# Four products of a block pair placed on four column quarters of TensorE, and small operands widened to all rows and columns

## The chip, the core and the metric

The kernel runs on one core of a Trainium2 chip. The metric is the device time of one execution in microseconds (us); of several runs the median is given. One execution was also recorded by the hardware profiler, and all durations below come from that record.

## What is computed

A two-layer graph network on 2708 nodes with 256 features. `adj` is 2708 x 2708, with about 3 in 1000 entries set near the average column and many more for the first nodes. Layer 0 (diagonal of the adjacency taken out as `dn`):

```python
node_support = node_adj_norm @ h
edge_output = _gru_cell(node_support, h, ...)
# per head:
hW = h @ W
hp = (node_adj > 0).astype(hW.dtype) @ hW
hm = (node_adj < 0).astype(hW.dtype) @ hW
e_plus = jax.nn.leaky_relu(jnp.concatenate([hp, hm], axis=1) @ a, ALPHA)[:, 0]
att = softmax(where(edge_adj > 0, e_plus[None, :], NEG_INF), axis=1)
out_head = att * edge_adj @ hW          # three heads, averaged
node_output = _gru_cell(edge_support, h, ...)
x = _layernorm(x + de[:, None] * edge_output + dn[:, None] * node_output)
```

Layer 1 is a graph attention of four heads over the entries of `adj` above 0.5 (`alpha = softmax(leaky_relu(s_src + s_dst), axis=0)`, `out = einsum(alpha, h)`), again with a residual and a layer norm.

## The kernel before

The nodes are cut into 22 blocks of 128 (the last has 20) and six groups of 512 columns (the last has 148). Everything is written as a list of operations that a planner (`Plan`, lines 99 to 276) orders by itself: each operation gets a cost (`cost`, line 151) and a `table`. On ScalarE that is an activation table; on TensorE, line 218, it is 1 for f32 operands and 2 for bf16. When the planner picks the next operation of an engine, one of another table counts as less urgent by `STAY` (5 us on TensorE) and costs `SWITCH` (0.13 us) more. Consecutive TensorE calls into the same tile are joined to one operation (`note`, line 192), up to 16. The order on each engine's queue, SP's and GpSimd's too, is the one that `issue` (line 230) finds. All instructions carry line 219 in the profile, so they are told apart by tile names.

The work goes in three stages.

*The pass* (lines 874 to 942) reads the transposed adjacency once, for each of the six groups in 11 pairs of blocks, 128 rows x 512 columns each. For a pair, ScalarE writes `over2` (sign of entry - 0.5) and `mask2` (sign of the entry, diagonal taken out by GpSimd), VectorE finds which 64-column pieces hold entries (`found0`). TensorE then makes four bf16 products: for each block b, `only[:, b, :]` (22 columns, a one in column b) with `over2`, summed into bank `dbs[0]` (`pf`), and `u3[:, b, :]` (9 columns: three heads in three bf16 parts) with `mask2`, into bank `accs[0]` (`pe`). At the end of a group, `logits` copies `pe` to `e9` and transposes it by a product with `sum3`; `flags` compares `pf` with `least` into `into` and transposes that with `ident_h`. Both read the banks that the next group writes. In between, `keep` (line 855) makes f32 products of x with the recurrent weights (`w_hs`), 128 x 512, into banks `accs[1]` and `dbs[1]` and stores them to `f_XH`; `listed` and `spread` turn the found blocks into index lists by bf16 products (`ls`, `pl` from `ids`). GpSimd gathers columns of the adjacency by these lists. After the last group, `head_weights` writes the exponentials into `f_T` (T0), and only then can rows be gathered from there.

*Layer 0* (lines 1238 to 1249) goes over 43 column blocks of 64. For each of some 181 gathered tiles GpSimd fetches `rows`, ScalarE scales the adjacency tile into `four` (three heads and the plain one) and writes its sign into `m0`, TensorE multiplies `rows` with `four` in f32 (`multiplied`) into `sums`, and every four tiles makes four small bf16 products of `m0` (64 columns) with 9 weights into `dens`. `divided` sums these, inverts them, spreads them over 64 x 192 (`rden_own`) and multiplies with `ones_f`, from 64 rows. After each group of 512 columns, `cells_and_norm` runs the GRU cells in f32 (`side`), the norm, and `projected` for layer 1.

*Layer 1* (lines 1401 to 1405) gathers from `f_T1` and is not touched.

What sets the order around the change: `over` and `mask` have three buffers each, the adjacency pairs five or six, so ScalarE's activations wait for TensorE's products three pairs back, and SP's loads for ScalarE and VectorE.

Of the kernel before, what the change touches and what calls it, by code (L numbers as in the profile page):

```python
# [20 lines left out]
P = 128  # L21
# [77 lines left out]
class Plan:  # L99
# [51 lines left out]
    def cost(self, engine, method, out, ins, kwargs):  # L151

        n = max(self.count(v) for v in [out] + ins)
        if method == "indirect_dma_start":
            return 1.25, 4.5
        if method == "dma_start":
            size = 4
            for _, k in tuple(out.ap):
                size *= k
            return 0.08 if engine == "sync" else 0.25, self.LOAD + size / self.RATE  # L160
        if engine == "tensor":
            n, rows = self.count(out), ins[0].ap[-1][1]
            if ins[0].dtype == BF16:
                t = max(0.035, n / 2400)
            elif method == "transpose":
                t = 0.11
            else:
                t = max(0.22 if rows <= C1 + 1 else 0.26, n / 595)
            return t, t + 0.1
        by_partition = any(isinstance(kwargs.get(k), bass.AP) for k in ("bias", "scale"))  # L170
        if engine == "scalar":
            t = 0.09 + n / 1200 + 0.1 * by_partition
        elif engine == "gpsimd":
            t = 0.1 + n / (1300 if method == "memset" else 320)
        elif method == "reciprocal":
            t = 0.07 + n / 160
        else:
            pairs = all(v.dtype == BF16 and tuple(v.ap)[-1] == (1, 2) for v in [out] + ins)
            t = 0.06 + n / (1900 if pairs else 3800 if method == "memset" else 960)
            t += 0.065 * (method == "scalar_tensor_tensor")  # L180
        return t, t + 0.08

    def note(self, engine, method, f, args, kwargs):
# [33 lines left out]
        if engine == "tensor":  # L217
            table = 1 + (ins[0].dtype == BF16)
        call = lambda: f(*args, **kwargs)  # L219
# [89 lines left out]
def fast_path(ctx: ExitStack, tc: tile.TileContext, i: dict, out: bass.AP, bad: bass.AP):  # L309
# [107 lines left out]

    only = const.tile([P, NB, NB], BF16, name="f_only")
    nc.gpsimd.memset(only, 0.0)
    for b in range(NB):  # L420
        nc.gpsimd.memset(only[:, b, b : b + 1], 1.0)

# [27 lines left out]
    for t, of in ((less_room, TILES0 + TILES1), (less_whole, WHOLE0 + WHOLE1)):  # L450
# [7 lines left out]

    least = const.tile([NB, 1], F32, name="f_least")
    nc.vector.tensor_scalar(  # L460
        least, ident[:NB, last : last + 1], float(P - size[last]), 0.5 - P, op0=ALU.mult, op1=ALU.add
    )

    sum3 = const.tile([H3, HEADS0], F32, name="f_sum3")
    nc.vector.tensor_add(sum3, ident[:H3, 0:3], ident[:H3, 3:6])
    nc.vector.tensor_add(sum3, sum3, ident[:H3, 6:9])
    sum9 = const.tile([H3, HEADS0], F32, name="f_sum9")
    nc.vector.tensor_scalar(sum9, sum3, float(HEADS0), None, op0=ALU.mult)

# [130 lines left out]
    def spread(layer, cs, rows, row_f, place):  # L600
# [29 lines left out]
        for b in range(NB):  # L630
            p = size[b]
            nc.tensor.matmul(
                pl[: 2 * rows * n, : n * PLACES], lhsT=lhs[:p, b // 2, b % 2], rhs=hot[:p, :, b // 2, :, b % 2],
                start=(b == 0), stop=(b == last),
            )
# [59 lines left out]
    ap, tiles = Rings(const, 1, home2), Rings(const, 8, home1)  # L695
    u3 = ap.tile([P, NB, H3], BF16, name="f_u3")
    e_col = const.tile([P, NB, HEADS0], F32, name="f_e_col")
# [93 lines left out]
    def logits(g, pe):  # L791

        e9 = ap.tile([H3, CH], F32, name="e9", bufs=2)
        w, bl = width[g], groups[g]
        nc.scalar.copy(e9[:, :w], pe[:H3, :w])
        pc = side()
        for n, b in enumerate(bl):
            nc.tensor.matmul(
                pc[: size[b], n * HEADS0 : (n + 1) * HEADS0],
                lhsT=e9[:, n * P : n * P + size[b]], rhs=sum3, start=True, stop=True,  # L800
            )
        full = sum(size[b] == P for b in bl)
        v = pc[:, : len(bl) * HEADS0].rearrange("p (b h) -> p b h", h=HEADS0)
        if full:
            nc.vector.tensor_copy(e_col[:, bl[0] : bl[0] + full, :], v[:, :full, :])
        if full < len(bl):
            nc.vector.tensor_copy(e_col[: size[last], last:, :], v[: size[last], full:, :])
# [20 lines left out]
    def flags(g, pf):  # L828

        into = ap.tile([NB, CH], BF16, name="into", bufs=2)  # L830
        w, bl = width[g], groups[g]
        nc.vector.tensor_scalar(into[:, :w], pf[:NB, :w], least, None, op0=ALU.is_gt)
        pt = side()
        for n, b in enumerate(bl):
            nc.tensor.matmul(
                pt[: size[b], n * NB : (n + 1) * NB], lhsT=into[:, n * P : n * P + size[b]],
                rhs=ident_h[:NB, :NB], start=True, stop=True,
            )
        full = sum(size[b] == P for b in bl)
        v = pt[:, : len(bl) * NB].rearrange("p (b c) -> p c b", c=NB)  # L840
        if full:
            nc.vector.tensor_copy(flags1[:, :, bl[0] : bl[0] + full], v[:, :, :full])
        if full < len(bl):
            p = size[last]
            nc.vector.tensor_copy(flags1[:p, :, last:], v[:p, :, full:])
# [28 lines left out]
    for g, cs in enumerate(groups):  # L874
        w = width[g]
        pe, pf = accs[0], dbs[0]
        c0, nf = base[g] // W0, w // W0
        for b0 in range(0, NB, 2):
# [30 lines left out]
            for p, s in parts:  # L909
# [7 lines left out]
                if nf * W0 < w:  # L917
# [4 lines left out]
                    )  # L922
            for b in pair:
                p = size[b]
                nc.tensor.matmul(
                    pf[:NB, :w], lhsT=only[:p, b, :], rhs=over2[:p, b - b0, :w], start=(b == 0), stop=(b == last)
                )
            for b in pair:
                p = size[b]
                nc.tensor.matmul(  # L930
                    pe[:H3, :w], lhsT=u3[:p, b, :], rhs=mask2[:p, b - b0, :w], start=(b == 0), stop=(b == last)
                )
        logits(g, pe)
        flags(g, pf)
        if g == NG - 3:
# [32 lines left out]

    COUNTED = 4
    gp, zp = Rings(const, 2, home1), Rings(const, 1, home2)  # L970

# [21 lines left out]
    def prepared(n):  # L993
# [16 lines left out]
        for h in range(HEADS0):  # L1010
            nc.scalar.activation(four[:, (h + 1) * w : (h + 2) * w], a, AF.Copy, scale=weight[:, h : h + 1])
        m0 = sp.tile([P, W0], BF16, name="m0", bufs=2 * COUNTED)
        nc.scalar.activation(m0[:, :w], a, AF.Sign)
# [11 lines left out]
    def multiplied(n):  # L1025
# [10 lines left out]
        for o in range(KD):  # L1036
# [3 lines left out]
            )  # L1040
        counted.append((start, stop, m0[:, :w], e3))
        if stop or len(counted) == COUNTED:
            for first_of, last_of, mask, weights_of in counted:
                nc.tensor.matmul(
                    dens[c][:w, :H3], lhsT=mask, rhs=weights_of, start=first_of, stop=last_of,
                    skip_group_check=True,
                )
            counted.clear()
# [5 lines left out]
    def divided(c):  # L1054
# [4 lines left out]
        acc = sums[c]  # L1059
        rden = small.tile([W0, HEADS0], F32, name="rden")[:w]  # L1060
        rb = small.tile([P, HEADS0 * W0], F32, name="rb")[:, : HEADS0 * w]
        own = small.tile([W0, HEADS0, W0], F32, name="rden_own")[:w, :, :w]

        if at == 0:
            zs[g] = (
                zp.tile([P, KD, CH], F32, name="sa", bufs=2), zp.tile([P, HEADS0, KD, CH], F32, name="z")
            )
        none = small.tile([W0, HEADS0], F32, name="none0")[:w]
        nc.vector.tensor_reduce(
            rden, dens[c][:w, :H3].rearrange("p (s h) -> p h s", s=3), AX.X, ALU.add  # L1070
        )
# [8 lines left out]
        nc.vector.tensor_mul(  # L1080
            own, ident[:w, :w].rearrange("p (o i) -> p o i", o=1).to_broadcast([w, HEADS0, w]),
            rden.rearrange("p (h o) -> p h o", o=1).to_broadcast([w, HEADS0, w]),
        )
        pb = dens[c][:, P : P + HEADS0 * w]
        nc.tensor.matmul(pb, lhsT=ones_f[:w], rhs=own, start=True, stop=True, skip_group_check=True)
        nc.scalar.copy(rb, pb)
# [6 lines left out]
    def cells_and_norm(g):  # L1093
# [87 lines left out]
        def projected(b):  # L1181
# [9 lines left out]
            of_head = ah[:, :H65].rearrange("p (h c) -> p h c", h=HEADS1)  # L1191
            s = small.tile([P, 2 * HEADS1], F32, name="s_d")[:p]
            nc.vector.tensor_scalar(s, ph[:p, D : D + 2 * HEADS1], REACH1, -REACH1, op0=ALU.min, op1=ALU.max)
            nc.scalar.activation(of_head[:, :, C1 :], s[:, :HEADS1].rearrange("p (h o) -> p h o", o=1), AF.Exp)
            nc.scalar.activation(ah[:, H65:], s[:, :HEADS1], AF.Exp, scale=SLOPE - 1.0)
            nc.tensor.transpose(pd[:HEADS1, b * P - c0 : b * P - c0 + p], s[:, HEADS1:], ident[:p, :p])
            nc.vector.tensor_mul(
# [19 lines left out]

        pd = dbs[1] if g == NG - 1 else ls_bank()
        for b in bl:
            projected(b)  # L1220
        S = small.tile([HEADS1, CH], F32, name="S", bufs=1)
        nc.scalar.activation(S[:, :w], pd[:HEADS1, :w], AF.Exp, scale=1.0 - SLOPE)
# [638 lines left out]
```

## Time and profile before

| | |
|---|---|
| three runs, us | 877.8, 881.07, 885.95 (median 881.07) |
| profiled execution | 877.66, its span 875.8 |
| matmuls on TensorE, busy | 780.4 us (89%), 3911 instructions |
| weight loads | 490.4 us (56%) |
| VectorE, ScalarE, GpSimd busy | 609.9 (70%), 551.3 (63%), 532.3 (61%) |
| GpSimd's gathers of `rows` | 254, 258.0 us, 1.016 each |
| f32 products of `rows` with `four` | 712 records, mean 400 ns |
| bf16 products of the pass | 132 into `acc`, 132 into `db` |

In the trace each f32 product shows as two matmul records. [...] two neighbours overlap and the sum of durations is more than the time they take; the distance from one start to the next is the better measure. "128*22" in a row is the product's rows and columns of weights, "128x512" the operand that streams through. "[idle <-X]" and "<-X" name what ended a wait. The stages meet at about 225 us (last column sums of the pass) and 700 us (last cells of layer 0).

### The profile page before, as it was taken

What the parts mean: (1) busy time and instruction counts of PE and PEld (TensorE: products, weight loads), DVE (VectorE), ACT (ScalarE), POOL (GpSimd) and SP (SyncE); (2) the same over time, 40 slices, a digit from 0 to 9 for tenths busy, and PEclk for the clock granted to TensorE, in tenths of its full rate; (3) what the DMA queues carried; (4) which work ended last, traced back from release to release, by engine and by line L of the source; (5) the groups of instructions that cost most, each with busy time, mean ns of one, the idle gap of its engine ahead of it and who ended that gap; (6) DMA issues with size and microseconds to landing.
All of it is one profiled execution on the core that took longest, in us unless ns stands there. A gap on an engine that the chain in (4) does not pass through costs nothing. (4 is left out here: it accounts for less than half of the span.)

```text
span 875.8 us, 14092 instructions
## 1 busy us (share of the span) xinstructions
PE 780.4 (89%) x3911; PEld 490.4 (56%) x3911; DVE 609.9 (70%) x2063; ACT 551.3 (63%) x1560; POOL 532.3 (61%) x613
## 2 busy tenths in 40 slices
PE   4999998997999999988998997999999899998882
PEld 3533333444556764656555744754664588777761
DVE  6259585865846674978478638727857849999993
ACT  3368997975568885658456844745764432237887
POOL 3000557557667777777777777777776243677630
PEclk9989999998999999989999999999999799999995
DMA  9476887878683342453446425434534143565531
GB/s 345 135 236 209 277 263 241 288 242 243 204 235 98 106 128 56 135 147 105 112 143 198 126 65 159 126 96 118 159 103 123 29 141 94 172 187 171 169 98 53
DMA packets 88503, 138.71 MB, mean 158 GB/s; under 512 B 21904, under 2 KB 44264, under 8 KB 87776
## 3 DMA queue, kind: packets, MB, share of 16 engines
q1 hardware_dynamic: 67168, 90.56, 32.2%
q0 software_dynamic: 20320, 45.59, 19.7%
q10 hardware_dynamic: 928, 1.57, 0.5%
q8 instruction: 33, 0.54, 0.3%
q14 instruction: 54, 0.44, 0.2%
HBM read 116.18 MB, written 24.26 MB: 160 GB/s over the span
## 5 line engine op out<-in xcount | busy, mean ns | idle before, releaser
L219 POOL DMA_INDIRECT rows<-f_T,f_idx x254 | 258.0, 1016 | 115.9 <-PE acc L219 26.8
L219 PE MATMUL acc<-four,rows 128*128 128x256 f32 (+1 forms) x712 | 187.9, 400 | 8.8 <-ACT four L219 5.7
L219 ACT ACTIVATE four<-four,rows 128x64 f32<-128x64 f32 (+1 forms) x534 | 143.3, 336 | 23.0 <-DMA rows<-f_T,f_idx 15.8
L219 PEld LDWEIGHTS acc<-four,rows 128*128 128x128 f32 x712 | 131.6, 196 | 45.8 <-ACT four L219 14.2
L219 POOL DMA_INDIRECT raw<-in_adj_dram,f_idx x91 | 90.5, 995 | 40.7 <-DVE f_m L219 15.3
L219 POOL DMA_INDIRECT f_xn<-in_adjT_dram,f_idx x63 | 66.8, 1060 | 20.1 <-issue 16.6
L219 POOL DMA_INDIRECT f_home<-in_adjT_dram,f_idx x67 | 66.4, 991 | 20.3 <-issue 16.3
L219 PE MATMUL acc<-f_home,rows 128*65 128x128 f32 (+2 forms) x512 | 65.2, 279 | 3.9 <-ACT f_home L219 2.6
L219 DVE TENSOR_TENSOR f_home<-f_home,side 128x512 f32<-128x512 f32 (+1 forms) x64 | 41.9, 658 | 32.4 <-PE side L219 31.2
L219 PEld LDWEIGHTS acc<-f_home,rows 128*65 128x65 f32 (+1 forms) x512 | 55.7, 140 | 9.6 <-ACT f_home L219 3.5
L219 PE MATMUL side<-f_home,f_gat_w 128*128 128x512 f32 (+1 forms) x144 | 58.7, 569 | 2.0 <-DVE f_home L219 1.9
L219 PE MATMUL side<-f_home,f_node_wi 128*128 128x512 f32 (+1 forms) x144 | 59.1, 543 | 1.3 <-DVE f_home L219 1.3
L219 ACT ACTIVATE m<-four 128x64 bf16<-128x64 f32 (+1 forms) x181 | 40.2, 246 | 28.1 <-DVE four L219 24.0
L219 PE MATMUL side<-f_home,f_edge_wi 128*128 128x512 f32 (+1 forms) x144 | 57.4, 544 | 0.0
L219 DVE SCALAR_TENSOR_TENSOR f_home<-pl,rows,f_m 128x128 f32<-128x128 f32 x196 | 55.2, 335 | 0.0
L219 POOL DMA_INDIRECT f_m<-in_adjT_dram,f_idx x33 | 31.9, 967 | 37.3 <-DVE f_rel L219 20.1
L219 PE MATMUL db<-f_home,rows 128*65 128x128 f32 x376 | 48.8, 282 | 6.3 <-DVE f_home L219 4.0
L219 DVE SCALAR_TENSOR_TENSOR f_home<-ls,rows,f_m 128x128 f32<-128x128 f32 (+1 forms) x168 | 46.3, 331 | 2.8 <-DMA rows<-f_T,f_idx 1.7
L219 PEld LDWEIGHTS db<-f_home,rows 128*65 128x65 f32 x376 | 39.0, 137 | 13.9 <-DVE f_home L219 5.9
L219 DVE TENSOR_REDUCE f_found<-f_home 128x16 f32<-128x1024 f32 (+8 forms) x52 | 43.7, 860 | 3.3 <-POOL f_home L219 3.3
L219 ACT ACTIVATE f_home<-f_home,f_minus_half 128x1024 bf16<-128x1024 f32 (+5 forms) x44 | 41.9, 965 | 5.8 <-PE db L219 4.1
L219 PEld LDWEIGHTS side<-f_home,f_gat_w 128*128 128x128 f32 x144 | 28.0, 208 | 30.1 <-issue 27.1
(231 smaller groups left out, 1537.3 us busy)
## 6 DMA issues: line engine op xcount, KB each, us to landing
f_home<-in_adjT_dram SPq DMA_DIRECT2D x30, 512.0 KB
f_XH<-kept SPq DMA_DIRECT2D x60, 256.0 KB
f_home<-f_XH SPq DMA_DIRECT2D x60, 256.0 KB
f_node_wi<-in_adjT_dram SPq DMA_DIRECT2D x10, 512.0 KB
f_edge_wi<-in_adjT_dram SPq DMA_DIRECT2D x10, 512.0 KB
f_home<-f_TS SPq DMA_DIRECT2D x5, 1024.0 KB
rows<-f_T SPq DMA_DIRECT2D x33, 132.0 KB
rows<-f_T,f_idx POOLq DMA_INDIRECT x254
```

The source lines that it names most:

```text
L219: call = lambda: f(*args, **kwargs)
```

## The change

The four products of a pair go into one bank, each into its own 32 partitions: `over2` of the even and the odd block into the first and the second quarter, `mask2` of the two into the third and fourth. The weights get 32 columns: `only` becomes a window of one tile, so that the block pair's number picks the column, and `u3` is padded with zeros. The bank alternates between the groups. `logits` and `flags` read all 128 partitions; `sum6` adds six columns where `sum3` added three, and `flags` picks the two quarters by a view of `ident_h`. In layer 0, `m0` is 128 columns wide, the upper half zero, `dens` gets 128 rows, and `divided` works on 128 partitions, so `rden_own` has 128 rows. `spread` multiplies all 128 rows of the last block. `projected` leaves its transposes into `pd` until all four blocks are through. The planner counts a product as `table` 2 if its weights have at most 64 columns or rows, and takes a quarter of the bf16 time for up to 32 columns.

```diff
-                t = max(0.035, n / 2400)
+                t = max(0.035, n / 2400) / (4 if rows <= P // 4 else 1)
...
-            table = 1 + (ins[0].dtype == BF16)
+            table = 1 + (self.count(ins[0]) <= P // 2 or tuple(ins[0].ap)[0][1] <= P // 2)
...
+    QUARTER = P // 4
+    only_any = const.tile([P, 2 * QUARTER], BF16, name="f_only")
+    nc.gpsimd.memset(only_any, 0.0)
+    nc.gpsimd.memset(only_any[:, QUARTER : QUARTER + 1], 1.0)
+    only = lambda k: only_any[:, QUARTER - k : 2 * QUARTER - k]
...
-                pl[: 2 * rows * n, : n * PLACES], lhsT=lhs[:p, b // 2, b % 2], rhs=hot[:p, :, b // 2, :, b % 2],
+                pl[: 2 * rows * n, : n * PLACES], lhsT=lhs[:, b // 2, b % 2], rhs=hot[:, :, b // 2, :, b % 2],
...
-    u3 = ap.tile([P, NB, H3], BF16, name="f_u3")
+    u3 = ap.tile([P, NB, QUARTER], BF16, name="f_u3")
+    nc.vector.memset(u3, 0.0)
...
-        nc.scalar.copy(e9[:, :w], pe[:H3, :w])
+        nc.scalar.copy(e9[:, :w], pe[:, :w])
...
-                lhsT=e9[:, n * P : n * P + size[b]], rhs=sum3, start=True, stop=True,
+                lhsT=e9[:, n * P : n * P + size[b]], rhs=sum6, start=True, stop=True,
...
-        nc.vector.tensor_scalar(into[:, :w], pf[:NB, :w], least, None, op0=ALU.is_gt)
+        nc.vector.tensor_scalar(into[:, :w], pf[:, :w], least, None, op0=ALU.is_gt)
...
-        pe, pf = accs[0], dbs[0]
+        sums_of = (accs[0], dbs[0])[g % 2]
...
-            for b in pair:
-                p = size[b]
+            for q, (lhs, rhs) in enumerate(
+                [(only(b0 // 2), over2[:, s, :w]) for s in range(2)]
+                + [(u3[:, b, :], mask2[:, b - b0, :w]) for b in pair]
+            ):
+                p = size[pair[q % 2]]
                 nc.tensor.matmul(
-                    pf[:NB, :w], lhsT=only[:p, b, :], rhs=over2[:p, b - b0, :w], start=(b == 0), stop=(b == last)
+                    sums_of[q * QUARTER : (q + 1) * QUARTER, :w], lhsT=lhs[:p], rhs=rhs[:p],
+                    start=(b0 == 0), stop=(b0 + 2 == NB),
                 )
-            for b in pair:
-                p = size[b]
-                nc.tensor.matmul(
-                    pe[:H3, :w], lhsT=u3[:p, b, :], rhs=mask2[:p, b - b0, :w], start=(b == 0), stop=(b == last)
-                )
...
+    m0s = const.tile([P, 2 * COUNTED, P], BF16, name="f_m0")
+    nc.gpsimd.memset(m0s[:, :, W0:], 0.0)
...
-        counted.append((start, stop, m0[:, :w], e3))
+        counted.append((start, stop, m0[:, : P if w == W0 else w], e3))
...
-        own = small.tile([W0, HEADS0, W0], F32, name="rden_own")[:w, :, :w]
+        own = small.tile([P, HEADS0, W0], F32, name="rden_own")[:p, :, :w]
...
-        nc.tensor.matmul(pb, lhsT=ones_f[:w], rhs=own, start=True, stop=True, skip_group_check=True)
+        nc.tensor.matmul(pb, lhsT=ones_f[:p], rhs=own, start=True, stop=True, skip_group_check=True)
...
-            s = small.tile([P, 2 * HEADS1], F32, name="s_d")[:p]
+            s = small.tile([P, 2 * HEADS1], F32, name="s_d", bufs=GR)[:p]
+            logits_of.append((b, s))
...
-            nc.tensor.transpose(pd[:HEADS1, b * P - c0 : b * P - c0 + p], s[:, HEADS1:], ident[:p, :p])
...
+        for b, s in logits_of:
+            p = size[b]
+            nc.tensor.transpose(pd[:HEADS1, b * P - c0 : b * P - c0 + p], s[:, HEADS1:], ident[:p, :p])
```

## The prediction

> **What bounds the kernel now.** I read the page first (TensorE's matmuls busy 89% of the span, no other engine above 70%), then the busy time of the engines in five stretches: the start of the pass, the rest of it, the first and second half of layer 0, and layer 1. Columns: stretch, length, then busy time (and instructions) of TensorE's matmuls, its weight loads, VectorE, ScalarE, GpSimd; granted clock, DMA share, GB/s.
>
> ```profile
> 0.00:60.00 60.00, 43.77 (x150) 25.23 (x151) 29.34 (x100) 28.72 (x31) 7.48 (x78) 0.96 0.71 245
> 60.00:225.00 165.00, 152.85 (x705) 65.40 (x703) 111.24 (x255) 130.28 (x188) 89.38 (x101) 0.96 0.79 246
> 225.00:465.00 240.00, 224.94 (x1120) 145.51 (x1121) 164.77 (x542) 159.16 (x560) 184.55 (x180) 0.97 0.47 132
> 465.00:700.00 235.00, 217.58 (x805) 133.01 (x805) 158.93 (x523) 138.87 (x465) 163.90 (x164) 0.96 0.41 119
> 700.00:876.00 176.00, 141.30 (x1134) 121.25 (x1134) 145.66 (x647) 94.23 (x318) 87.04 (x91) 0.93 0.45 135
> ```
>
> TensorE is the fullest engine up to 700 us. In layer 1 it is VectorE, and the change leaves layer 1 nearly alone. Who keeps ScalarE waiting in the pass (0 to 225 us; total, times, longest)?
>
> ```profile
> ACT f_home L219 <- PE acc L219: 13.3, 6, 5.0
> ACT kept L219 <- PE acc L219: 12.0, 2, 11.5
> ...
> ACT got L219 <- PE pl L219: 8.9, 2, 7.5
> ACT f_home L219 <- PE db L219: 5.9, 2, 4.1
> ```
>
> That is 40 us of waiting for TensorE, against 159 us of ScalarE's own work (28.7 + 130.3). So the pass is paced by TensorE, with ScalarE close behind. Then I looked at TensorE's timeline for distances from start to start, which say more than the overlapping durations.
>
> ```profile
> 171.21 0.59 PE L219 MATMUL acc<-f_home,f_home 128*9 128x512 bf16 x2
> 171.64 0.59 PE L219 MATMUL db<-f_home,f_only 128*22 128x512 bf16 x2
> 172.16 1.99 PE L219 MATMUL db<-f_xT,f_node_wh 128*128 128x512 f32 x4
> 173.99 1.88 PE L219 MATMUL acc<-f_xT,f_edge_wh 128*128 128x512 f32 x4
> 175.79 0.60 PE L219 MATMUL db<-f_home,f_only 128*22 128x512 bf16 x2
> ...
> 287.88 2.86 PE L219 MATMUL acc<-four,rows 128*128 128x256 f32 x12
> 290.67 0.59 PE L219 MATMUL db<-rden_own,f_ones_f 64*128 64x192 f32 x2
> 291.18 1.13 PE L219 MATMUL acc<-four,rows 128*128 128x256 f32 x4
> ```
>
> Two products of 9 or 22 columns take 0.43 us, 0.215 each, one after the other, though each fills a quarter of the columns or less. From them to an f32 product of all columns it is 0.52 instead of 0.43: 0.09 is lost. Below, twelve products of 0.216 take 2.79 instead of 2.59, and the two of 64 rows take 0.51 instead of 2 x 0.16. Around each change of shape 0.09 is lost in leaving, and 0.10 after the first f32 product, whose successor waits for its weights.
>
> **What the Trainium skill says.** TensorEngine Tiling (Array Packing), section Key Properties: changing the tiling mode drains TensorE, and different tiles run in parallel. The trace agrees on the drain, with the 0.09 us above. TensorE: Matmul & The Clock Gate, section Part 3: three products on three column groups gave 2.38 times the rate, and the output's first partition picks the group. The trace has one such case:
>
> ```profile
> 83.53 0.38 PE L219 MATMUL acc<-f_home,f_home 128*9 128x512 bf16 x1
> 83.54 0.19 PE L219 MATMUL ls<-f_row_of,got 128*32 128x16 bf16 x3
> 83.75 0.38 PE L219 MATMUL acc<-f_home,f_home 128*9 128x512 bf16 x1
> ```
>
> Three small products, each to another quarter of the output's partitions, start 0.01 us after a 512-column one and don't hold up the next, which is again 0.22 behind. So quarters do run side by side, at least with 16 columns. Four of 512 at once appear nowhere.
>
> **Part by part.**
>
> *The four products.* 110 + 110 products of 512 columns and 22 + 22 of 148. In the first 30 us the clock is cold: six take 2.56 us, 0.427 each; I counted 34 such distances. So 186 x 0.216 + 34 x 0.427 + 44 x 0.064 = 57.5 us. After: 55 pairs of 512 and 11 of 148. From below, one stream each: 57.5 / 4 = 14.4. From the skill's rate: 0.216 x 3 / 2.38 = 0.27 for three, so 57.5 x 0.27 / 0.216 / 4 = 18 (an estimate from that page). From above: no overlap, 57.5. I take 17.5, a saving of **40 us**. The last pair of a group holds a block of 20 rows and will not overlap: 6 times under 0.6 us, inside the rounding.
>
> *Changes of shape.* In the timeline I counted neighbouring matmuls whose rows or columns fall in different classes (up to 32, up to 64, all): 147 before 225 us, 212 in 225 to 700. With the denominators' mask padded to 128 columns, `rden_own` on 128 rows, the spread's last block on all rows, and `sum6` and `into` on 128 rows, 20 and 162 of them go. For `rden_own`: 43 blocks, each 0.09 + 0.10 + 0.09 + 0.10 = 0.38, together 16; I take 15, as some stand beside other changes. Denominator batches: 28 returns to the f32 products at 0.09 + 0.09 and 0.04 of the late weights (they are partly late after any bf16 product) is 6. Spread: 11 times two drains, 2. So **23 us** of TensorE time in layer 0, and 2 in the pass. The 64 added mask columns cost nothing that I can see: weight loads of 64 columns took 111 ns and those of 128 columns in the spread 102.
>
> *One bank per group, in turn.* Group g+1 no longer waits until `logits` and `flags` have emptied the banks: ScalarE waited 2.0 us for its 9x512 copy at the first of the five boundaries. It is part of the 40 us above.
>
> *Bigger operands on other engines.* `e9`, `into`, `rden`, `none`, `own` get more partitions and the same elements on each; these rows (9x512 copy 0.57, 22x512 compare 0.73) cost what full ones do (128x512 copies 0.57 and 0.68). Nothing. At the start 22 GpSimd memsets (0.8 us) go, and a VectorE memset and one on GpSimd come (memsets of that size in the timeline: 0.2 to 0.5 us); GpSimd idles from 14.6 us, and the first pair waits for its transfer.
>
> *The order.* The planner no longer counts f32 against bf16 but small against full shapes, and takes a quarter of the time for the four products. All instructions may move. The denominators and the spread lose the planner's reluctance to leave f32; the four products keep it (5 us of urgency, against keeps). The `s_d` transposes go behind all four blocks of `projected`: they need a ring of four and delay `S` by at most the last block's path, 5 or 6 times under 1 us, beside the other blocks' work. DMAs: none added or removed. SP's loads come when buffers come free, so earlier. What the new order costs I cannot read from the trace; I allow 12 us to either side.
>
> **What arrives at the end.** The pass: TensorE gives back 42 us, but ScalarE has 159 us of work and 14 us before its first tile, and the DMA share times length is 0.71 x 60 + 0.79 x 165 = 173 us, at the best share seen in a 25 us stretch (0.95) 182 us. So the pass can't fall from 225 below 185; 40 is the ceiling. Waits that now lie in TensorE's shadow (keeps' copies that hold up SP's queue, ScalarE behind VectorE's lists) come out. I take 22 of 40. Layer 0: of 23 us I take 13, because GpSimd is nearly as full: its gathers start 1.25 us apart (1.0 busy, 0.25 to 0.30 issue), and 344 instructions x 1.25 = 430 of the 475 us. But 91 of all gathers fetch layer 1's masks as filling, and the last ones for layer 0 start at 649 us while TensorE's last product is at 692, so it leads. Sum: 35 us. The profiled execution took 877.66 us (span 875.8 and 1.9 around it); the median of the runs is 881.07, 3.4 more. 877.7 - 35 + 3.4 = **846 us**.
>
> **Rivals.**
>
> *All of it arrives* (16%): 40 us in the pass and 15 in layer 0: 826. For: ScalarE waits 40 us for TensorE. Against: DMA would have to run at its best share all through.
>
> *Another engine has the pace* (13%): the pass turns out to hang on DMA and SP's order, layer 0 on GpSimd; 8 us remain: 873. For: 0.79 DMA share, gathers end to end. Against: the waits above.
>
> *Slower* (9%): the pairs' products are held back. They are now one step that needs both masks and the `u3` of both blocks, where the two `over` products could go ahead, and they alone are the small shape, so the planner runs keeps (1.8 us each) first. `over` and `mask` have three buffers; a product one keep late stops ScalarE, then the loads. It decides once the hold exceeds 35 / 55 = 0.64 us a pair: one more keep before every second pair is 27 x 1.8 = 49, less 35: 895. Against: a pair's product is the most urgent work in the pass, and ScalarE has slack for part of it.
>
> *No overlap of four streams of 512 columns* (6%; the change then doesn't do what it says): 40 us of the TensorE saving go, layer 0's 13 and a few for the banks remain: 865.
>
> **Numbers.** The likeliest course (56%) gives 846. The range 822 to 873 leaves out the slower case, half of the 873 case and the far side of the best. A change under about 1% can't be told from none here: the three runs spread by 8 us. Faster by over 1% (under 872): the likeliest, the first and last rival and part of the second, 0.83. Within 1%: 0.08. Slower: 0.09.
>
> **What will show it.** Right: four products of a pair start within some 0.02 us and the next pair's or the keep's product 0.22 to 0.3 later; products with `rden_own` and the masks show 128 rows and columns and no extra 0.09 or 0.10 around them; ScalarE's waits for TensorE before the pass's end fall well under 40 us; the first `rows` gather, at 236 us before, comes near 214; layer 0's last product comes some 13 us earlier still, relative to it. Wrong: starts 0.2 us apart within a pair; the first `rows` gather still at 236 with a DMA share near 0.8; GpSimd without gaps while TensorE waits for `rows`; ScalarE waiting longer for `acc` or `db` than before.

## The result, and the profile after

The changed kernel took 841.77 us (median of four runs, 840.51 to 845.8) against 880.58 for the kernel before beside it (four runs): a ratio of 0.956, 95% interval 0.9504 to 0.9616. Its profiled execution took 842.26 us, the one before 877.66: 35.4 us less, where the prediction's sum had 35, and the median is 4 us under the predicted 846. But the time did not come from where the prediction looked for it. First the busy time by stretch, with the columns that the prediction named.

```profile
0.00:60.00 60.00, 41.21 (x166) 24.61 (x166) 30.60 (x104) 29.94 (x34) 7.11 (x59) 0.89 0.77 261
60.00:225.00 165.00, 139.13 (x736) 61.35 (x736) 125.25 (x295) 136.02 (x210) 117.63 (x128) 0.93 0.84 254
225.00:465.00 240.00, 224.31 (x1174) 154.04 (x1175) 169.46 (x552) 169.39 (x613) 167.14 (x165) 0.98 0.49 138
465.00:700.00 235.00, 220.32 (x960) 145.71 (x959) 169.02 (x573) 129.41 (x418) 163.71 (x170) 0.98 0.44 121
700.00:840.00 140.00, 107.83 (x878) 91.95 (x876) 119.69 (x543) 81.92 (x289) 70.44 (x74) 0.90 0.47 139
```

In the second line, TensorE's matmuls fall from 152.9 to 139.1 us while every other engine does more than before: VectorE 125 (was 111), ScalarE 136 (130), GpSimd 118 (89). The pass has become a little shorter and a good deal fuller. TensorE's granted clock fell there from 0.96 to 0.93. The clock of the first line can't be compared: the clock record of a trace begins late (at 42.1 us before, at 33.9 us after), and the view counts the time ahead of it as full clock, although the prediction found products at twice their distance there (0.427 us). ScalarE's waits up to 225 us:

```profile
ACT f_home L219 <- issue: 11.4, 4, 3.9
...
ACT kept L219 <- PE acc L219: 9.1, 1, 9.1
...
ACT f_home L219 <- PE db L219: 4.8, 1, 4.8
...
ACT f_home L219 <- PE acc L219: 2.4, 2, 1.5
ACT got L219 <- PE pl L219: 2.1, 1, 2.1
```

The rows that name TensorE come to 19.5 us (9.1 + 4.8 + 2.4 + 2.1, and two of 0.9 and 0.2 that are not shown), where they were 40. The row of 11.4 us, which no record explains, is new. TensorE's timeline shows the new products, in the pass and in layer 0.

```profile
166.61 3.37 PE L219 MATMUL acc<-f_xT,f_node_wh 128*128 128x512 f32 x4 [1.19 <-ACT kept L219]
...
177.98 0.39 PE L219 MATMUL acc<-f_home,f_only 128*32 128x512 bf16 x2
177.99 0.39 PE L219 MATMUL acc<-f_home,f_home 128*32 128x512 bf16 x2
178.21 0.38 PE L219 MATMUL acc<-f_home,f_only 128*32 128x512 bf16 x2
...
178.83 0.39 PE L219 MATMUL acc<-f_home,f_only 128*32 128x512 bf16 x2 [0.23 <-ACT f_home L219]
179.77 0.39 PE L219 MATMUL acc<-f_home,f_home 128*32 128x512 bf16 x2 [0.55 <-ACT f_home L219]
...
286.21 0.22 PE L219 MATMUL db<-rows,f_m 128*128 128x9 bf16 x3
...
287.89 0.59 PE L219 MATMUL db<-rden_own,f_ones_f 128*128 128x192 f32 x2 [0.21 <-DVE rden_own L219]
288.32 2.75 PE L219 MATMUL acc<-four,rows 128*128 128x256 f32 x12
```

Four products of 512 columns begin within 0.01 us and the next pair 0.23 after the first (177.98 to 178.21); one after the other they took 0.86. The four start together only if all their operands are ready: so it is in 33 of the 50 pairs of full blocks. In the other 17 the second two come 0.1 to 1.5 us later, as at 179.77, where they wait for ScalarE. From four that started together to a product of full shape it is 0.33 us (median of 15, from 60 to 225 us), so leaving the small shape still costs some 0.1. The denominators' products now show 128 rows and columns, and from `rden_own` to the next product it is 0.43 for its two records; the median over the 43 blocks is 0.325, where it was 0.52.

The stages as the traces show them (us; "gathers" counts GpSimd's indirect transfers that began before 225 us; "changes" counts neighbouring matmuls of another class of rows or columns, in the whole kernel):

| | before | after |
|---|---|---|
| last column sum of the pass | 224.2 | 216.2 |
| first `rows` gather | 236.0 | 230.8 |
| last product of `rows` with `four` | 692.0 | 651.1 |
| from the first line to the third | 467.8 | 434.8 |
| gathers before 225 us | 79 | 106 |
| gathers between the first line and the third | 337 | 309 |
| changes of shape | 378 | 170 |

The pass gave 8 us and layer 0 gave 33. What follows layer 0's last product gave back some 5 (189.2 us instead of 183.8). Predicted were 22, 13 and nothing.

### The profile page after: what moved, and what is told of

It is laid out like the page before. It is cut to its first block, busy times and chain, and to the rows that moved or that the text cites. A ratio compares the mean times of both kernels' runs of the same rounds, so it can differ in the third digit from the quotient of the medians.

```text
span 840.3 us, 14025 instructions
## 1 busy us (share of the span) xinstructions
PE 732.8 (87%) x3911; PEld 477.7 (57%) x3911; DVE 614.0 (73%) x2062; ACT 546.7 (65%) x1560; POOL 526.0 (63%) x593
## 4 chain that ended last, share of the span: by engine, by line
PE 20%; DVE 17%; ACT 9%; DMA 4%; issue 3%; POOL 0%; SPq 0%; DVEq 0%; ACTq 0%
PE side L219 13%; DVE f_home L219 12%; PE acc L219 5%; DMA raw<-in_adj_dram,f_idx 3%; ACT y L219 2%; ACT f_home L219 2%; PE db L219 2%; ACT four L219 2%; DVE f_xn L219 1%; ACT f_xn L219 1%; DMA rows<-f_T,f_idx 1%; DVE ids L219 1%; ACT L219 1%; DVE four L219 1%; PE pl L219 0%
## 5 line engine op out<-in xcount | busy, mean ns | idle before, releaser
L219 POOL DMA_INDIRECT rows<-f_T,f_idx x254 | 252.4, 994 | 124.2 <-ACT four L219 32.1
L219 PE MATMUL acc<-four,rows 128*128 128x256 f32 (+1 forms) x712 | 180.0, 389 | 8.6 <-ACT four L219 3.8
L219 PEld LDWEIGHTS acc<-four,rows 128*128 128x128 f32 x712 | 129.0, 191 | 38.8 <-issue 13.0
L219 POOL DMA_INDIRECT f_home<-in_adjT_dram,f_idx x67 | 68.5, 1022 | 19.8 <-issue 15.0
L219 POOL DMA_INDIRECT f_xn<-in_adjT_dram,f_idx x63 | 63.7, 1011 | 18.3 <-issue 16.7
L219 PE MATMUL side<-f_home,f_gat_w 128*128 128x512 f32 (+1 forms) x144 | 55.6, 542 | 1.2 <-DVE f_home L219 1.2
L219 ACT ACTIVATE f_m<-four 128x64 bf16<-128x64 f32 (+1 forms) x181 | 40.7, 246 | 12.3 <-DVE four L219 10.3
L219 PEld LDWEIGHTS db<-f_home,rows 128*65 128x65 f32 x376 | 41.3, 142 | 11.7 <-DVE f_home L219 4.1
L219 DVE TENSOR_SCALAR f_m<-raw 128x128 uint8<-128x128 f32 (+1 forms) x91 | 20.8, 241 | 34.8 <-DMA raw<-in_adj_dram,f_idx 34.6
```

## Experiments

Eight of the runs were on two chips on which every kernel, the one before too, took some 17 to 19% longer (1029.08 and 1032.76 us for the kernel before). The engines' own work was the same there (in the changed kernel GpSimd was busy for 525.5 us, elsewhere for 526.0); the time went into idle stretches of up to 13.5 us that no recorded instruction or transfer ended, and why is not known. These runs are read as ratios to the kernel before on the same chip, and even the ratio does not carry over: the changed kernel's is 0.9714 there and 0.956 elsewhere, with intervals that do not meet. The rule alone, the old price, the cut stores and the second series run were on chips where the kernel before took 880.89 and 880.35 us.

**Are the wide denominators worth anything?** The changed kernel was run again for comparison (`a1_after`). Then it ran with the denominators narrow again, in its own order (the planner was told the wide shape), twice; and the kernel before with nothing but the widening (and `only` as one small tile, for room), in its own order on TensorE, ScalarE and SP.

```diff
-        counted.append((start, stop, m0[:, : P if w == W0 else w], e3))
+        counted.append((start, stop, m0[:, :w], e3))
...
-        p = P if w == W0 else w
+        p = w
```

> The changed kernel itself, beside the kernel before and the three below on one chip, as the measure for them: ratio 0.95 to 0.962 of the kernel before if the gain is a share of the time on any chip.

> The changed kernel with the denominators narrow again (mask 64 columns, dens and rden_own on 64 rows), and every engine's order of instructions exactly that of the changed kernel. Shape theory: the removed drains and late weights are what layer 0 gained, so this gives back most of the 23 us worked out, 18 to 26 us: 860 to 868 us, with layer 0 (from the first product of four to the last, 436 us after the change, 463 before) longer by as much. Order theory: layer 0 gained by the planner's other order and by gathers done ahead in the pass, and the narrow shapes hide behind GpSimd: 2 to 8 us, 844 to 850.

> Narrow denominators in the changed kernel's order, now beside the changed kernel. Shape theory: slower than the changed kernel by 18 to 26 us (2.1 to 3% of the kernel before). Order theory: by 2 to 8 us.

> The kernel before with only the denominators widened (mask 128 columns, dens and rden_own on 128 rows), in the order of the kernel before. Shape theory: 20 us of TensorE time go and most arrives: 0.975 to 0.983 of the kernel before. Order theory: layer 0 is paced by the order and by the gathers, so the freed time turns into waits: 0.99 to 1.0.

Measured: the changed kernel 0.9714 (0.963 to 0.9799), outside the expected 0.95 to 0.962; narrow 0.9779 (0.9691 to 0.9866) and 0.9787 (0.9732 to 0.9842); the old kernel widened 0.9972 (0.993 to 1.0015). The narrow form has 332 changes of shape against 170 and costs 0.7%, within the intervals; the widened old kernel has 247, where the kernel before had 378 in its trace, and gains 0.3%, which can't be told from none. By these intervals the shapes are worth at most some 15 us, and they are not where 33 us come from. All of this was measured on the slower chips, whose idle stretches may hide a part. On the others there is a sign only: with the new rule and narrow denominators layer 0 takes 454.4 us, and with the new rule, wide denominators and the old price 453.7 (both runs are below).

**Do the quarters pay?** Each of the four products gets 128 columns of weights, three quarters of them zero, and sums into the whole bank; the four run one after another. The planner is told the quarters' price and shape, so that the order stays nearly that of the changed kernel.

```diff
-                [(only(b0 // 2), over2[:, s, :w]) for s in range(2)]
-                + [(u3[:, b, :], mask2[:, b - b0, :w]) for b in pair]
+                [(only(s * QUARTER + b0 // 2), over2[:, s, :w]) for s in range(2)]
+                + [(u3_all[:, b, :], mask2[:, b - b0, :w]) for b in pair]
...
-                    sums_of[q * QUARTER : (q + 1) * QUARTER, :w], lhsT=lhs[:p], rhs=rhs[:p],
+                    sums_of[:, :w], lhsT=lhs[:p], rhs=rhs[:p],
```

> The changed kernel with the four products of a pair each on all 128 columns of one bank, so one after the other with no change of shape; the planner is told the quarter costs, so that the order stays nearly the same. If the pass is still paced by TensorE, its 40 us of saved time come back in the pass, less some 130 drains of 0.09 us: pass end 216 to about 245, total 865 to 870. If the pass is now paced by ScalarE, VectorE and the transfers, most is hidden: pass end 220 to 228, total 845 to 855.

> The changed kernel with the four products of a pair one after another, each on all 128 columns and into the whole bank (the other three quarters of its weights are zero), told to the planner at the same price and as the same shape, so that the order is nearly that of the changed kernel: some 40 us more of TensorE in the pass. Theory (after the change TensorE no longer sets the pass, so that the quarters' 40 us are worth little by themselves): within 0.7% of the changed kernel's 0.956, so 0.949 to 0.963, with the pass's last product within 5 us of the changed kernel's 216 us. Rival (the quarters' 40 us do pay, and an earlier run of this form hid it because every kernel of that run had idle time that nothing explains): 0.97 to 0.985, with the pass's last product 10 to 25 us later than 216 us.

Measured: 0.9705 (0.9618 to 0.9793) the first time, and 0.9515 (0.9473 to 0.9556), 839.09 us, the second, with the pass's last product at 213.4 us. The theory holds: without the quarters the kernel is no slower. Whether it is faster can't be said, since its interval overlaps that of the changed kernel. Its timeline and then its stretches, the second time:

```profile
174.09 0.81 PE L220 MATMUL acc<-f_home,f_home 128*128 128x512 bf16 x3
...
175.09 2.75 PE L220 MATMUL acc<-f_home,f_home 128*128 128x512 bf16 x12
177.68 1.02 PE L220 MATMUL acc<-f_xT,f_edge_wh 128*128 128x512 f32 x2
```

```profile
0.00:60.00 60.00, 42.06 (x179) 25.60 (x182) 36.04 (x129) 34.03 (x38) 9.59 (x63) 0.95 0.80 268
60.00:225.00 165.00, 148.14 (x734) 71.82 (x743) 123.06 (x283) 132.30 (x205) 118.56 (x125) 0.99 0.84 255
```

Twelve products take 2.59 us (175.09 to 177.68), 0.216 each: nothing overlaps. Yet TensorE is only 9 us busier from 60 to 225 us. Two reasons can be read, which do not cover the whole difference. In this form there are 52 changes of shape before 225 us where the changed kernel has 115, since full columns follow full columns; at the 0.09 us that the prediction read for leaving a shape, that is 6 us. And the clock: from 60 to 225 us it is 0.99 here and 0.93 with the quarters. Two groups of the keeps' f32 products show it. The changed kernel first, groups from 60 to 225 us (busy, mean ns):

```profile
L219 PE MATMUL acc<-f_xT,f_node_wh 128*128 128x512 f32 x48 | 28.5, 724 | 5.6 <-DVE kept L219 4.0 <-ACT kept L219 1.5
L219 PE MATMUL db<-f_xT,f_node_wh 128*128 128x512 f32 x48 | 27.7, 707 | 2.9 <-DVE kept L219 1.6 <-ACT kept L219 1.4
```

The series form:

```profile
L220 PE MATMUL db<-f_xT,f_node_wh 128*128 128x512 f32 x48 | 24.8, 642 | 3.6 <-ACT kept L220 1.8 <-DVE kept L220 1.7
L220 PE MATMUL acc<-f_xT,f_node_wh 128*128 128x512 f32 x46 | 22.9, 619 | 2.4 <-DVE kept L220 1.5 <-ACT kept L220 0.8
```

These products take 707 to 724 ns with the quarters and 619 to 642 without; the keeps' other two groups, with `f_edge_wh`, do not differ (606 and 615 ns against 603 and 608). From start to start (60 to 225 us), 19 of 135 distances of all four groups are over 0.6 us with the quarters, 3 of 137 in series, and 5 of 132 in the kernel before; above their normal 0.43 us all distances sum to 10.2, 3.5 and 5.1 us. The trace's clock record shows half clock in these places. The four at 166.61 above, after 1.19 us without work, are such a case: 3.37 us for four. The Trainium skill, TensorE: Matmul & The Clock Gate, section "What's actually happening", says that the gate halves the clock after an idle window of some 3.4 us. The traces agree with the halving, 0.43 to 0.85 us from start to start, but not with the condition: in the changed kernel half clock came five times between 60 and 225 us, and the longest pause of TensorE in the 3.4 us before was only 0.4 to 1.6 us. The other runs below fit: the two further traces with quarters (the old price, the cut stores) have 23 and 12 of some 137 distances over 0.6 us, the rule alone 8 of 135. So part of the time that the quarters free, some 7 us of the keeps' products, goes back as half clock; that the pauses cause it is argued, not tested.

**Is it the planner's rule for a change of shape?** First the changed kernel with the old rule, twice, then the kernel before with the new rule and nothing else; there the narrow denominators are told to the planner as full.

```diff
-            table = 1 + (self.count(ins[0]) <= P // 2 or tuple(ins[0].ap)[0][1] <= P // 2)
+            table = 1 + (ins[0].dtype == BF16)
```

> The changed kernel with the planner's old rule (f32 against bf16) for when TensorE changes over. Order theory: the new rule is worth 15 us or more, so 857 or above. Shape theory: the operands give the gain whatever the order, so within 6 us of the changed kernel, 838 to 848.

> The old rule for TensorE's changes, now beside the changed kernel; the first look had it slower than the kernel before. Order theory: the rule carries the gain of layer 0, so slower than the changed kernel by 30 us or more, and the part from the first product of four to the last is where they differ. Shape theory: within 6 us of the changed kernel, and the first look was the chip.

> The kernel before with nothing but the planner's rule for a change of shape as in the changed kernel: a product counts as one of another shape only if its weights or its rows are 64 or fewer, and the denominators' products, still 64 wide in the machine, are told to the planner as full. The four products of a pair, their price and every operand are as before. Theory (the new rule's order carries layer 0's gain): 0.965 to 0.985 of the time before; the stretch from the first to the last product of weighted sums about 20 to 40 us shorter than the 572 us that the widened denominators at the old order had on such a chip, and the pass's last product unchanged within 3 us of 240 us. Rival (the order is worth something only together with the wide operands or the quarters): 0.99 to 1.01, and the stretch 560 to 580 us. Rival (the rule alone is slower, because it now mixes f32 and bf16 freely while the narrow operands still cost their changes): over 1.01.

Measured: with the old rule 1.0208 (1.0114 to 1.0301) and 1.0165 (1.0038 to 1.0292), so all of the change but this line is slower than no change, and some 5% above the changed kernel's 0.9714. (Only on the slower chips; the second figure rests on two runs.) Of the difference, 43 us lie between the first and the last product with `four`: 572.8 us in the first of these runs, 529.4 in the changed kernel on the other of the two chips. With the new rule alone 0.9824 (0.9752 to 0.9895), 867.19 us beside 880.89: 13.7 us for an edit that alters no product. The stretches of the rule alone:

```profile
60.00:225.00 165.00, 154.93 (x708) 66.20 (x707) 113.93 (x262) 133.31 (x200) 91.98 (x102) 0.96 0.83 250
225.00:465.00 240.00, 225.51 (x1122) 143.36 (x1122) 163.53 (x532) 156.99 (x557) 182.27 (x178) 0.98 0.47 131
465.00:700.00 235.00, 222.45 (x852) 136.57 (x851) 161.78 (x534) 141.78 (x468) 167.68 (x168) 0.98 0.44 121
```

The pass is that of the kernel before (154.9 us of TensorE, GpSimd at 92; its last product at 223.9). From there to layer 0's last product it is 454.4 us instead of 467.8: 13.4 less, with 406 changes of shape, 28 more than before. The expected 20 to 40 us were for the slower chips. This gain is one of order alone. Under the old rule a product of the other type counted as 5 us less urgent, under the new one f32 and bf16 of full shape mix freely; which waits in layer 0 this ended was not followed further.

**And the price of a quarter?** The changed kernel, with the four products priced as before.

```diff
-                t = max(0.035, n / 2400) / (4 if rows <= P // 4 else 1)
+                t = max(0.035, n / 2400)
```

> The changed kernel with the planner's price of the pass's four products and of other products with 32 or fewer columns of weights not divided by four; the machine's products are those of the changed kernel, only the order can differ. Theory (the rule for changes of shape carries the order's gain, the price little): within 0.7% of the changed kernel, which gave 0.971 of the kernel before here, so 0.964 to 0.979. Rival (the price of a quarter is what lets the pass's work move forward): 0.985 to 1.0, with the pass's last product 8 us or more later than 248 us.

Measured: 0.9663 (0.959 to 0.9736), 851.16 us: inside the theory's range, but 1.1% above the changed kernel's 0.956, and the pass moved against the rival's sign. The stretches:

```profile
60.00:225.00 165.00, 136.31 (x665) 58.52 (x664) 115.40 (x264) 125.28 (x192) 92.11 (x102) 0.92 0.85 255
225.00:465.00 240.00, 219.02 (x1173) 149.50 (x1171) 168.21 (x542) 167.24 (x597) 181.84 (x180) 0.99 0.47 132
```

GpSimd is at 92 us from 60 to 225 us, near the 89 of the kernel before. The pass ends at 205.6 us, 18.6 before the old one and 10.7 *before* the changed kernel's, and layer 0 takes 453.7 us. The price thus makes the pass longer and layer 0 shorter (the last two columns: gathers that began between the two products, and the median, with the kernel before at 880.35 to 880.89 beside each):

| | pass's last product | from there to layer 0's last | gathers before 225 us | gathers in layer 0 | time, us |
|---|---|---|---|---|---|
| before | 224.2 | 467.8 | 79 | 337 | 880.58 |
| new rule alone | 223.9 | 454.4 | 81 | 329 | 867.19 |
| changed, old price | 205.6 | 453.7 | 86 | 327 | 851.16 |
| changed | 216.2 | 434.8 | 106 | 309 | 841.77 |
| changed, in series | 213.4 | 435.5 | 108 | 309 | 839.09 |

With the lower price the planner puts the lists and their gathers earlier: 20 more before 225 us, which at the prediction's 1.25 us from gather to gather is 25 us of GpSimd's time taken out of layer 0. That fits the 19 us by which layer 0 is shorter; it is argued from the counts, not tested alone. The counts fit the other rows too: layer 0 takes 1.38 to 1.41 us for each gather in it in all five, so its length goes with the count of GpSimd's gathers. If they have the pace there, that would also explain why wider denominators, quicker on TensorE, do not shorten it.

The table leaves one step unexplained. Between the rule alone and the old price the pass loses 18.3 us and the time falls by 16. The quarters, the turn of banks, the widened operands and the order that follows from them all lie in this step, and no run takes the four products apart at the old price. The medians of the two prices, 851.16 and 841.77, were not taken side by side; their ratios are 0.9663 and 0.956, with intervals that overlap at 0.959 to 0.9616, so the sign of the price's worth is likely but not settled.

**One bank or two in turn?**

```diff
-        sums_of = (accs[0], dbs[0])[g % 2]
+        sums_of = accs[0]
```

> The changed kernel with all six groups summed in one bank. If the turn of banks matters, five boundaries cost about 2 us each: 848 to 854. If the groups' ends are hidden by keeps, 841 to 844.

Measured: 0.9761 (0.9675 to 0.9847) against the changed kernel's 0.9714; not resolved. The pass's last product came at 260.9 us, against 248.3 in the changed kernel on such a chip (and 248.0 in the narrow form on the same chip): 12.6 us of the pass, of which little reaches the end.

**What sets the pass now?** The stores of the kept tiles cut to a quarter of their columns, in the changed kernel's order.

```diff
-        nc.sync.dma_start(place_kept(g, n, o, gate), t)
+        nc.sync.dma_start(place_kept(g, n, o, gate), t[:, : width[g] // 4])
```

> The changed kernel with each stored tile of the cells (512 columns, 60 of them) cut to its first 128 columns when it is stored, so that the pass moves some 11.8 MB less; read back, those 128 columns are repeated four times. The order of all engines is that of the changed kernel. What is left out: three quarters of the cells' kept products, so the output is not the reference's. Theory (after the change the pass has the DMA's pace, 84% of it busy from 60 to 225 us): the pass's last product 15 us or more earlier than the 248 us that the changed kernel showed on such a chip, and the time 0.945 to 0.96 of the kernel before. Rival (ScalarE has the pace, 136 of 165 us busy): the pass's last product within 4 us of 248 us, and the time 0.965 to 0.975.

Measured: 0.9571 (0.95 to 0.9641), 844.37 us, with the pass's last product at 214.4 us, against 216.2. The expectation's 248 us and 0.971 were those of the slower chips, so that the ratio lies in the theory's range is no sign for it: beside the changed kernel's 0.956 nothing was gained. Its line, 60 to 210 us:

```profile
60.00:210.00 150.00, 123.97 (x667) 53.22 (x667) 111.92 (x253) 126.22 (x180) 105.93 (x116) 0.95 0.72 204
```

The changed kernel's:

```profile
60.00:210.00 150.00, 125.17 (x664) 53.64 (x664) 111.92 (x255) 126.16 (x181) 105.38 (x116) 0.93 0.83 255
```

The DMA share falls from 0.83 to 0.72 and the pass ends 1.8 us earlier. So neither the amount that the DMA moves nor, by the series form, TensorE has the pace of the pass. ScalarE and TensorE are the fullest, at 126 and 125 of 150 us, and neither is full. What sets the pass now, ScalarE's work, the order of the loads or the sequence in which the engines hand over to each other, stays open; no run lightened ScalarE or moved the loads.

## Why the prediction was right, and where its steps were not

The number and the sum (35 us) were right; the account behind them was not. Terms that were too large and terms that were too small, or missing, came out nearly even, and that is luck.

*The four products: saving 40.* The overlap was read rightly from three small products, and so was its size: 17.5 of 57.5 us is 0.26 for four, and 0.23 to 0.33 was measured where they start together. (Of the 34 distances at half clock the trace shows some 26, under 2 us in the sum.) But the step from TensorE's time to the kernel's fell: the series form gives none of this overlap and is as fast. "The pass is paced by TensorE" does not hold in the changed kernel's order; in the order of the kernel before it was not tested.

*The pass: 22 of 40; layer 0: 13 of 23.* These are the terms that were mis-sized: 8 and 33 were measured, and 5 were given back behind layer 0, for which the sum had no term. With the old price they would have been nearly met (18.6 and 14.1 in that run). The planner, told that the products are cheap, then spent some 10 us of the pass on lists for layer 0 and shortened that by 19. No term of the sum had work moving between the stages. The step "TensorE leads" in layer 0 is doubtful too, since the stage's length goes with the count of gathers.

*Changes of shape: 23 us.* The count was nearly right (182 predicted to go, 208 gone), and TensorE's own cost too: `rden_own` and its successor are 0.2 us closer at the median of the 43 blocks. The worth for the kernel was not: widening alone gave 0.3%, narrowing cost 0.7%, both within what can't be told from none. The prediction's 13 us for layer 0 did appear, in the rule alone, without one widened operand: the right size for another reason.

*The order: "I allow 12 us to either side."* This is the step that failed. The order was no disturbance around the gain but carried much of it: 13.7 us came from the rule without any other edit, perhaps 9 more by the price, and with all other edits but the rule the kernel was 2% slower than before (on the slower chips). The 16 us between stay unassigned, as said. A line that changes what a planner counts can't be priced at nothing with a margin.

*One bank in turn: 2.0 us*, read from a single wait. The pass lost 12.6 us without it; at the end it is within the error.

*Bigger operands: nothing.* Agrees for the denominators: the old kernel with wide ones was not slower. `e9` and `into` were not tested alone.

*The rivals.* Held-back pairs did not come: ScalarE's waits for `acc` and `db` fell. Another engine at the pace was true in part: of the 40 us of TensorE, the pass gave 8, and layer 0 goes with GpSimd's gathers.

*What was to show it.* Starts (in 33 of 50 pairs), widths and ScalarE's waits (19.5 instead of 40 us) came as named. The first `rows` gather did not: 230.8 instead of near 214, with a DMA share of 0.84, close to a named sign of being wrong. It told that the pass was not where the gain lay.

## What to carry to other kernels

When a scheduler orders the instructions, an edit to its costs or rules is a change of its own: try it alone first, on the unchanged instructions, and try the faster instruction with the schedule held fixed. Here time freed on the fullest engine was worth only what the sequence of handovers let through, and a stage that gets only a little shorter may have taken on work of the next one: count the next stage's instructions inside it. An agreeing total is no proof of its terms.

## What the runs showed of the hardware

Four products of 512 columns on the four quarters of the columns started 3 to 4 ns apart and held up the next pair by 0.23 us in all, close to a quarter of the 0.86 us in series, and a product of full shape by 0.33. In the pass TensorE got half clock more often with the products overlapped: from 60 to 225 us for 24, 28 and 16 us in three traces with quarters, and for 13, 12 and 4 us in three without (before, rule alone, series), though its pauses just before were at most 1.6 us in the changed kernel. Over the whole execution the kernels before and after do not differ in this (granted clock 0.941 to 0.959 and 0.949 to 0.957). From the last of the masks' products to the next f32 product it was 25 ns at the median, bf16 to f32 with both of full shape, where the 64-column products of the kernel before took 105: the loss of some 0.08 us goes with the shape, not with the type.
